# Reordering the start of a tuned graph-attention kernel: projections ahead of the mask rows, later weight loads, and a wider split of the last rows

## The chip, the cores and the metric

The kernel runs on one core of one Trainium2 chip. The metric is the device time of the whole kernel in microseconds (us); the profile's span is some 1.8 us shorter than the time of the same execution. Every timed run below is in the fast state, but for the single run of before_again, whose state is unknown. Single executions of one and the same kernel still scatter over some 3 to 16 us, so the first results are quoted as a median with its lowest and highest, and the later ones as a ratio with its interval. TensorE is also called PE, VectorE DVE, ScalarE ACT, GpSimd POOL and SyncE SP.

## The reference

Sixteen graphs of 1024 nodes share one adjacency matrix. Each goes through three transformer blocks with masked attention and then one graph-attention layer. Cut to what matters:

```python
def block(adj, h, Wq, Wk, Wv, Wo, bo, ...):          # three times; 8 heads of 16
    Q, K, V = (h @ W split into heads for W in (Wq, Wk, Wv))
    scores = einsum('bnhd,bmhd->bhnm', Q, K) / sqrt(16)
    scores = where(adj == 0, -inf, scores)
    x = layernorm(h + softmax(scores) @ V @ Wo + bo)
    return layernorm(x + relu(x @ W1 + b1) @ W2 + b2)

def last(x, adj, W, a_src, a_dst, ...):
    h = x @ W
    e = leaky_relu((h @ a_src)[:, :, None] + (h @ a_dst)[:, None, :], 0.2)
    return layernorm(softmax(where(adj == 0, -inf, e)) @ h + x)
```

x is 16 x 1024 x 128 in float32, adj 1024 x 1024 in int32.

## The kernel before

The 16 graphs times 3 layers are 48 blocks. A block has 32 score steps: head group (2) x query half (2) x key tile (8). One step makes two PSUM slots of scores; ACT takes one (exponential, then a product with the 0/1 mask on POOL), VectorE the other (it adds the mask, then ACT does the exponential); in three of eight key tiles VectorE takes both. The key and query projections are kept as a high and a low part, which DMA copies stack in four interleaved rows ("stack"). The parts that the change touches:

```python
def slot(dtype=F32):                     # three of these, for scores
    return psum.tile([P, N], dtype, tag="s", name="s", bufs=3)
def bank():                              # one of these, for projections and the rest
    return psum.tile([P, 512], F32, tag="t", name="t", bufs=1)
...
W = [load_layer(nc, nc.sync, const, a, 0, ("Wq", "Wk"))]          # in 64 B pieces
W[0].update(load_layer(nc, nc.scalar, const, a, 0, ("Wv", "bo")))
...
for t in range(NT):                      # the eight mask rows are fetched at once
    ...
    nc.sync.dma_start(ai, adj[t * P:(t + 1) * P, :])
def masks(t):                            # one mask row: DVE, 8 transposes, DVE, ACT
    ai, ab = rows_in[t]
    nc.vector.tensor_scalar(ab, ai, 0.0, None, op0=OP.not_equal)
    ps = slot(BF16)
    for k in range(NT):
        nc.tensor.transpose(ps[:, k * P:(k + 1) * P], ab[:, k * P:(k + 1) * P], identb)
    psv = ps.rearrange("p (k q) -> p k q", q=P)
    nc.vector.tensor_copy(mask01[:, :, t * P:(t + 1) * P], psv)
    nc.scalar.activation(mask_add[:, :, t * P:(t + 1) * P], psv, AF.Identity, scale=-BLOCKED, bias=blocked, ...)
def first_weights():                     # layer 0's other weights: ACT issues them
    W[0].update(load_layer(nc, nc.scalar, const, a, 0, ("Wo", "b2", "W1", "b1", "W2", "ln1_g", "ln2_g")))
    norm_weights(nc.scalar, 0)
    add_bias(nc.scalar, "ln1_b", 0, "b2", 0)
...
def rows_gh():                           # in the last layer of each batch
    ...
    for r in range(2):
        queue = nc.scalar if r and b == B - 1 else nc.sync
        for i in range(4):
            queue.dma_start(g_rows[...], parts[...])
            queue.dma_start(h_rows[...], parts[...])
...
put(proj_tasks(0), ("proj", 0))          # the start
need(("proj", 0))
for t in range(NT):
    masks(t)
stack(0, 0)
first_weights()
fetch(1)()
...
for m, (b, l) in enumerate(blocks):
    order = [(g, qh) for g in range(G) for qh in range(2)]
    if m == len(blocks) - 1:
        order.sort(key=lambda x: x[1])
    for at, (g, qh, kt) in ...:
        if at == 1:
            stack(m, 1)
        if n == 3:
            other_weights()
        ...
        if at == 19:
            need(("proj", m + 1)); stack(m + 1, 0)
        e = score_step(step)
```

Of the kernel before, what the change touches and what calls it, by code (L numbers as in the profile page):

```python
# [9 lines left out]
F32 = mybir.dt.float32  # L10
# [8 lines left out]
P = 128  # L19
H = 8  # L20
HD = 16
G = 2
# [6 lines left out]
SOON = 120  # L29
LANES = 4  # L30
AHEAD = 4
BOTH_ON_DVE = (2, 5, 7)
# [27 lines left out]

def load_layer(nc, queue, pool, a, l, names):
    w = {}
    for n in names:
        src = a[f"L{l}_gnn_{n}"]
        if n in ("Wq", "Wk"):

            t = pool.tile([P, src.shape[1]], F32, name=f"{n}{l}")
            for g in range(G):
                queue.dma_start(t.rearrange("p (g j d) -> p g j d", g=G, j=J)[:, g],
                                src.rearrange("i (j g d) -> i g j d", g=G, j=J)[:, g])  # L70
        elif n == "b1":
            t = pool.tile([P, src.shape[0] // P], F32, name=f"{n}{l}")
            queue.dma_start(t, src.rearrange("(f p) -> p f", p=P))
        elif n == "W2":
            t = pool.tile([P, src.shape[0] // P, src.shape[1]], F32, name=f"{n}{l}")
            queue.dma_start(t, src.rearrange("(f p) d -> p f d", p=P))
        elif len(src.shape) == 2:
            t = pool.tile([P, src.shape[1]], F32, name=f"{n}{l}")
            queue.dma_start(t, src)
        else:  # L80
            t = pool.tile([P, src.shape[0]], F32, name=f"{n}{l}")
            queue.dma_start(t, rows_of(src))
        w[n] = t
    return w
# [22 lines left out]
def fast_path(ctx: ExitStack, tc: tile.TileContext, a: dict, out: bass.AP, flag):  # L107
# [13 lines left out]
    def slot(dtype=F32):  # L121

        return psum.tile([P, N], dtype, tag="s", name="s", bufs=3)

    def bank():

        return psum.tile([P, 512], F32, tag="t", name="t", bufs=1)

    def half_tile(name):
# [13 lines left out]
    state = {("x", 0): load_x(0)}  # L143
    W = [load_layer(nc, nc.sync, const, a, 0, ("Wq", "Wk"))]
    W[0].update(load_layer(nc, nc.scalar, const, a, 0, ("Wv", "bo")))
# [22 lines left out]
    for t in range(NT):  # L168
        if t < 6:
            ai = work.tile([P, 2, N], I32, tag="e", name="ai", bufs=6)  # L170
            ai, ab = ai[:, 0], ai.bitcast(BF16)[:, 1, :N]
        else:
            ai = work.tile([P, N], I32, tag="Wk", name="ai", bufs=4)
            ab = work.tile([P, N], BF16, tag="Wq", name="ab", bufs=4)
        nc.sync.dma_start(ai, adj[t * P:(t + 1) * P, :])
        rows_in.append((ai, ab))

    def masks(t):
        ai, ab = rows_in[t]
        nc.vector.tensor_scalar(ab, ai, 0.0, None, op0=OP.not_equal)  # L180
        ps = slot(BF16)
        for k in range(NT):
            nc.tensor.transpose(ps[:, k * P:(k + 1) * P], ab[:, k * P:(k + 1) * P], identb)
        psv = ps.rearrange("p (k q) -> p k q", q=P)
        nc.vector.tensor_copy(mask01[:, :, t * P:(t + 1) * P], psv)
        nc.scalar.activation(mask_add[:, :, t * P:(t + 1) * P], psv, AF.Identity, scale=-BLOCKED, bias=blocked,
                             saturate=False)
# [14 lines left out]
    def first_weights():  # L202
        W[0].update(load_layer(nc, nc.scalar, const, a, 0, ("Wo", "b2", "W1", "b1", "W2", "ln1_g", "ln2_g")))
        norm_weights(nc.scalar, 0)
        add_bias(nc.scalar, "ln1_b", 0, "b2", 0)

# [4 lines left out]
    def other_weights():  # L211
        for l in range(1, L):
            W.append(load_layer(nc, nc.sync, const, a, l, [n for n in LAYER if n not in ("ln1_b", "ln2_b")]))
            norm_weights(nc.sync, l)
            add_bias(nc.sync, "ln2_b", l - 1, "bo", l)
            add_bias(nc.sync, "ln1_b", l, "b2", l)
        nc.sync.dma_start(ln2_b_last, rows_of(a[f"L{L - 1}_gnn_ln2_b"]))
        for n in LAST:
            src = a[f"L3_gnn_{n}"]
            if n == "W":  # L220
                t = w_nodes[:, :D]
                nc.sync.dma_start(t, src)
            elif n in ("a_src", "a_dst"):
                t = const.tile([P, 1], F32, name=n)
                nc.sync.dma_start(t, src.rearrange("(p o) -> p o", o=1))
            else:
                t = const.tile([P, D], F32, name=n)
                nc.sync.dma_start(t, rows_of(src))
            wl[n] = t

    def last_weights():
# [19 lines left out]
    def soon():  # L251

        return tc.high_priority(offset=SOON)

# [76 lines left out]
    def proj_tasks(m):  # L331
# [39 lines left out]
        return [(2 if n in (3, 4, 5, 6) else 1, f, {0: "+w", 1: "+w", 6: "-w", 7: "-w"}.get(n, "")) for n, f in enumerate(pieces)]  # L371

    def stack(m, g):

        for n, order in (("Wk", (0, 1, 0, 1)), ("Wq", (0, 0, 1, 1))):
            for pp in range(2):
                t = work.tile([P, N], F32R, tag=n, name=n, bufs=4)
                r0 = (g * J + 2 * pp) * HD
                for i, part in enumerate(order):
                    nc.sync.dma_start(t[i:P:4, :].bitcast(F32), state[n, m][part][r0:r0 + 2 * HD, :].bitcast(F32))  # L380
                state[n, g, pp] = t
# [5 lines left out]
    def score_step(step):  # L387
# [3 lines left out]
        for pp in range(2):  # L391
# [9 lines left out]
            if on_pool:  # L401
                nc.scalar.activation(ev, psv, AF.Exp, scale=HD ** -0.5)  # L402
                nc.gpsimd.tensor_mul(ev, ev, m)  # L403
            else:
                nc.vector.tensor_add(ev, psv, m)  # L405
                masked.append((2 * step_no[0] + pp + (kt not in BOTH_ON_DVE), ev))
# [106 lines left out]
    def last_tasks(b):  # L513
# [39 lines left out]
        def rows_gh():  # L553
# [6 lines left out]
            for r in range(2):  # L560

                queue = nc.scalar if r and b == B - 1 else nc.sync
                for i in range(4):
# [103 lines left out]

    put(proj_tasks(0), ("proj", 0))
    need(("proj", 0))
    for t in range(NT):  # L670
        masks(t)
    stack(0, 0)
    first_weights()
    fetch(1)()

# [44 lines left out]
    with tc.manual_schedule(engines={mybir.EngineType.PE, mybir.EngineType.Activation}):  # L720
        for m, (b, l) in enumerate(blocks):
            order = [(g, qh) for g in range(G) for qh in range(2)]
            if m == len(blocks) - 1:
                order.sort(key=lambda x: x[1])
            for at, (g, qh, kt) in enumerate((g, qh, kt) for g, qh in order for kt in range(NT)):
                now[0] = n
                if at == 1:
                    stack(m, 1)
                if n == 3:
                    other_weights()  # L730
                if n == 40:
                    last_weights()
                if at == 0 and m + 2 < len(blocks) and blocks[m + 2][1] == 0:
                    put([(0, fetch(blocks[m + 2][0]), "+x")], ("fetch", blocks[m + 2][0]))
                if m + 1 < len(blocks):
                    if at == 6:
                        need(("post",) + (blocks[m + 1][0], blocks[m + 1][1] - 1) if blocks[m + 1][1] else
                             ("fetch", blocks[m + 1][0]))
                        put(proj_tasks(m + 1), ("proj", m + 1), first=True)
                    if at == 19:  # L740
                        need(("proj", m + 1))
                        stack(m + 1, 0)
                step = m, g, qh, kt
                e = score_step(step)
                waiting.append((step, e, n + AHEAD))
# [249 lines left out]
```

## Time and profile before

| | before |
|---|---|
| time on record for the prediction, median of 3 | 4124.35 us (4121.5 to 4125.04) |
| profiled execution, span | 4126.3 us, granted clock 0.985 |
| first score on TensorE | 41.99 us |
| first masked sum on VectorE | 45.38 us |
| accumulator mark 1 (first transpose of the accumulator, 8 steps) | 68.98 us |
| accumulator mark 8 (end of the second block) | 196.79 us |
| "parts" of the last batch but one to the end of the span | 70.6 us |

The marks are the lines `tt<-acc` of the DVE timeline: VectorE turns over the accumulator once in eight steps, so equal marks of two kernels show how far one is ahead. The other names are of the last layer: "parts" is the small tile from which the rows of g and h are copied, the edges are TensorE's products of these rows, and an aggregate is 128 matmuls of edge weights with node values (`t<-hd,e`). The page's totals say how busy the engines are over all (busy us, share of the span, instructions):

```profile
PE 3819.7 (93%) x44501; PEld 1548.1 (38%) x44501; DVE 3405.9 (83%) x5324; ACT 3393.8 (82%) x3961; POOL 3445.7 (84%) x3010
```

With TensorE 93% busy and the middle nearly untouched (only the order of the copies in `stack` changes there, in every block), only the first and the last 70 us are in play. The prediction shows and reads the other lines.

### The profile page before, as it was taken

Reading aid. Unit: us, or ns where it says so; the run is one execution under the profiler, and the core shown is the slowest. Engines: PE = TensorE matmul, PEld = TensorE weight load, DVE = VectorE, ACT = ScalarE, POOL = GpSimd, SP = SyncE. Lnnn points to the kernel's source line nnn. Section 1 sums busy time; section 2 is a strip of 40 time slices with the busy share of each in tenths; the row PEclk is TensorE's granted clock in tenths of the full one; section 3 lists DMA queues with packets and bytes.
Section 4 is the critical chain, followed back from the end, with each engine's and each line's share of the span. In section 5 each row is a group of like instructions: output and inputs, shape, how many; then the busy total and the mean of one; then the engine's idle time right before and its main releaser. Section 6 shows DMA issues by size and latency. Waiting matters only on the chain.

```text
span 4126.3 us, 107667 instructions
## 1 busy us (share of the span) xinstructions
PE 3819.7 (93%) x44501; PEld 1548.1 (38%) x44501; DVE 3405.9 (83%) x5324; ACT 3393.8 (82%) x3961; POOL 3445.7 (84%) x3010
## 2 busy tenths in 40 slices
PE   7999999999999999999999999999999999999996
PEld 2333333344443333334444333333444433333445
DVE  6888888888887888888888888888888888888874
ACT  6899999977778999997777899998777789999760
POOL 4788888887788888897878888888888888888885
PEclk9999999999999999999999999999999999999998
DMA  5221221222221222221222212221222212212100
GB/s 152 68 57 47 63 62 43 62 53 53 54 66 50 62 52 53 62 54 47 68 53 53 63 47 58 62 56 50 53 60 63 52 42 63 62 48 57 45 25 19
DMA packets 126289, 233.11 MB, mean 56 GB/s; under 512 B 36704, under 2 KB 75616, under 8 KB 125792
## 3 DMA queue, kind: packets, MB, share of 16 engines
q1 hardware_dynamic: 122896, 225.14, 21.7%
q8 instruction: 352, 5.77, 0.6%
q10 hardware_dynamic: 2896, 1.01, 0.1%
q14 instruction: 145, 1.19, 0.1%
HBM read 15.54 MB, written 8.39 MB: 6 GB/s over the span
## 4 chain that ended last, share of the span: by engine, by line
PE 47%; DVE 19%; ACT 12%; POOL 12%; issue 9%; DMA 1%; SPq 0%; ACTq 0%; DVEq 0%; POOLq 0%
PE t L271 18%; PE acc L422 15%; PE s L395 11%; DVE e L405 11%; POOL e L403 6%; ACT e L402 5%; ACT e L417 5%; DVE st L296 2%; PE t L260 2%; POOL x L315 2%; DVE lo L360 2%; DVE x L303 1%; ACT xT L265 1%; DVE tt L433 1%; POOL x L319 1%
## 5 line engine op out<-in xcount | busy, mean ns | idle before, releaser
L405 DVE TENSOR_TENSOR e<-s,mask_add 128x1024 f32<-128x1024 f32 x2112 | 2500.1, 1212 | 413.3 <-PE s L395 328.0
L417 ACT ACTIVATE e<-e 128x1024 f32<-128x1024 f32 x2112 | 2196.4, 1062 | 364.1 <-DVE e L405 341.2
L403 POOL TENSOR_TENSOR e<-e,mask 128x1024 f32<-128x1024 f32 x960 | 2049.3, 2150 | 395.4 <-ACT e L402 392.7
L422 PE MATMUL acc<-e,v 128*17 128x512 f32 x12288 | 1630.9, 603 | 64.0 <-DVE tt L433 32.9
L395 PE MATMUL s<-Wq,Wk 64*128 64x512 f32 x6144 | 1209.0, 459 | 80.3 <-ACT e L402 34.9
L402 ACT ACTIVATE e<-s 128x1024 f32<-128x1024 f32 x960 | 982.3, 1023 | 188.3 <-PE s L395 172.2
L395 PEld LDWEIGHTS s<-Wq,Wk 64*128 64x128 f32 x6144 | 499.1, 186 | 1069.1 <-DVE e L405 437.2
L422 PEld LDWEIGHTS acc<-e,v 128*17 128x17 f32 x12288 | 208.0, 95 | 581.4 <-issue 463.8
L315 POOL TENSOR_SCALAR x<-x,mv 128x128 f32<-128x128 f32 x896 | 389.2, 448 | 24.0
L319 POOL TENSOR_TENSOR x<-x,ln_g 128x1024 f32<-128x1024 f32 x97 | 229.3, 2364 | 28.8 <-PE t L260 28.8
L271 PE MATMUL t<-hd,e 128*32 128x129 f32 x8192 | 245.6, 277 | 7.3 <-DVE x L597 3.2
L313 POOL TENSOR_TENSOR mv<-mv,half_neg 128x4 f32<-128x4 f32 x224 | 231.9, 1035 | 18.5
L271 PEld LDWEIGHTS t<-hd,e 128*32 128x32 f32 x8192 | 227.4, 111 | 27.0 <-issue 5.2
L271 PE MATMUL t<-x1T,W 128*32 128x512 f32 x1536 | 203.5, 602 | 3.1 <-ACT x1T L265 1.6
L303 DVE TENSOR_TENSOR x<-t,x 128x512 f32<-128x512 f32 x192 | 131.8, 686 | 89.8 <-PE t L271 84.5
L260 PE MATMUL t<-identf,x 128*128 128x128 f32 x896 | 150.9, 292 | 55.4 <-DVE lo L360 27.4
L296 DVE BATCH_NORM_STATS2 st<-x 128x6 f32<-128x128 f32 x896 | 196.8, 279 | 3.0
L271 PEld LDWEIGHTS t<-W,hT 128*32 128x32 f32 x6144 | 171.4, 110 | 62.5 <-issue 26.5
L311 POOL TENSOR_SCALAR mv<-mv 128x4 f32<-128x4 f32 x224 | 52.8, 236 | 167.5 <-DVE mv L298 137.4
L260 PEld LDWEIGHTS t<-identf,x 128*128 128x128 f32 x896 | 97.0, 144 | 251.9 <-issue 96.5
L271 PE MATMUL t<-W,hT 128*32 128x128 f32 x6144 | 185.4, 273 | 2.7 <-DVE x L303 1.9
L582 DVE SCALAR_TENSOR_TENSOR e<-s,mask 128x1024 f32<-128x1024 f32 x128 | 150.6, 1210 | 5.9 <-PE s L579 4.8
(83 smaller groups left out, 2490.1 us busy)
## 6 DMA issues: line engine op xcount, KB each, us to landing
Wk<-hi SPq DMA_DIRECT2D x384, 128.0 KB
Wk<-lo SPq DMA_DIRECT2D x384, 128.0 KB
Wq<-hi SPq DMA_DIRECT2D x384, 128.0 KB
Wq<-lo SPq DMA_DIRECT2D x384, 128.0 KB
x<-in_x_dram SPq DMA_DIRECT2D x16, 512.0 KB
out_dram<-x SPq DMA_DIRECT2D x31, 256.0 KB
ai<-in_adj_dram SPq DMA_DIRECT2D x8, 512.0 KB
g_rows<-parts SPq DMA_DIRECT2D x124, 4.0 KB
```

Of the source, the lines that this page charges most:

```text
L260: nc.tensor.transpose(ps[:, t * P:(t + 1) * P], src[:, 4 * h + t, :], identf)
L271: nc.tensor.matmul(dst[j:j + SLOT, :], lhsT[:, j:j + SLOT], rhs, start=start, stop=stop)
L296: nc.vector.bn_stats(st[:, t, :], z[:, t, :])
L313: nc.gpsimd.tensor_tensor(v, v, half_neg[:, ts], OP.pow)
L315: nc.gpsimd.tensor_scalar(z[:, t, :], z[:, t, :], mv[:, t, 0:1], mv[:, t, 1:2], op0=OP.add, op1=OP.mult)
L319: nc.gpsimd.tensor_mul(z, z, rows(gain, n))
L395: nc.tensor.matmul(ps[:, r * 512:(r + 1) * 512], k[64 * r:64 * r + 64, kt * P:(kt + 1) * P], q[64 * r:64 * r + 64, q0:q0 + 512], start=Tru ...
L402: nc.scalar.activation(ev, psv, AF.Exp, scale=HD ** -0.5)
L403: nc.gpsimd.tensor_mul(ev, ev, m)
L405: nc.vector.tensor_add(ev, psv, m)
L417: nc.scalar.activation(ev, ev, AF.Exp, scale=HD ** -0.5)
L422: nc.tensor.matmul(acc[j * SLOT:j * SLOT + HD + 1, :], v_bufs[m % 2][:, kt, 2 * j + g, :], e[:, j, :], start=first, stop=last)
```

## The change

Its intent: start the scores sooner. ACT loses the early weight loads; the first block's projections come first, in the three score slots; scores start with half of the queries and so half of the mask rows; the other four mask rows are made inside steps 1 to 4; all other weights load later from SP. A side change gives ACT half of the g and h rows of the last batch but one, as before only of the last. The core of the diff:

```diff
     def bank():
+        if head[0]:
+            return slot()[:, :512]
         return psum.tile([P, 512], F32, tag="t", name="t", bufs=1)
...
-    W = [load_layer(nc, nc.sync, const, a, 0, ("Wq", "Wk"))]
+    raw = {n: work.tile([P, D], F32, tag="row", name=n, bufs=2) for n in ("Wk", "Wq")}
+    W = [load_layer(nc, nc.sync, const, a, 0, ("Wk", "Wq"), raw)]     # whole rows, DVE reorders
...
-        W[0].update(load_layer(nc, nc.scalar, const, a, 0, ("Wo", "b2", "W1", "b1", "W2", "ln1_g", "ln2_g")))
-        norm_weights(nc.scalar, 0)
-        add_bias(nc.scalar, "ln1_b", 0, "b2", 0)
+        W[0].update(load_layer(nc, nc.sync, const, a, 0, ("Wo", "b2", "W1", "b1", "W2", "ln1_g", "ln2_g")))
+        norm_weights(nc.sync, 0)
...
     def stack(m, g):
-        for n, order in (("Wk", (0, 1, 0, 1)), ("Wq", (0, 0, 1, 1))):
-            for pp in range(2):
+        for pp in range(2):
+            for n, order in (("Wk", (0, 1, 0, 1)), ("Wq", (0, 0, 1, 1))):
...
-                queue = nc.scalar if r and b == B - 1 else nc.sync
+                queue = nc.scalar if r and b >= B - 2 else nc.sync
...
-    put(proj_tasks(0), ("proj", 0))
-    need(("proj", 0))
-    for t in range(NT):
-        masks(t)
-    stack(0, 0)
-    first_weights()
-    fetch(1)()
+        load_rows(range(4))
+        put(proj_tasks(0), ("proj", 0))
+        need(("proj", 0))
+        stack(0, 0)
+        load_rows(range(4, NT))
+        fetch(1)()
+        ...                                     # masks of rows 0 to 3
+    head[0] = False
...
-            if m == len(blocks) - 1:
+            if m in (0, len(blocks) - 1):
                 order.sort(key=lambda x: x[1])
-                if at == 1:
+                if at == (6 if m == 0 else 1):
                     stack(m, 1)
-                if n == 3:
-                    other_weights()
+                if n == 6:
+                    with tc.issue_after(behind["stack"]):
+                        first_weights()
+                        other_weights()
+                if n == 20:
+                    with tc.issue_after(behind["pool"]):
+                        biases()
-                    if at == 19:
+                    if at == (24 if m == 0 else 19):
                         need(("proj", m + 1))
                         stack(m + 1, 0)
-                e = score_step(step)
+                if FIRST <= n < FIRST + 4:
+                    with tc.manual_schedule(engines={mybir.EngineType.DVE}):
+                        e = score_step(step)
+                        neighbours(4 + n - FIRST)
+                        masks(4 + n - FIRST, mask_rows(4 + n - FIRST))
+                else:
+                    e = score_step(step)
```

## The prediction

> **What bounds the kernel now.** I read the 40 slices first (the page), then busy time by stretches, then the timeline at both ends. The slices say that TensorE is full almost everywhere:
>
> ```profile
> PE   7999999999999999999999999999999999999996
> ACT  6899999977778999997777899998777789999760
> ```
>
> Only the first slice (103 us) and the last have slack, and the change edits just these two. In between nothing moves: one block of 32 score steps lasts 217.18 to 293.31 us = 76.1 us between equal marks (the transposes of the accumulator), with TensorE busy 71.6 of them:
>
> ```profile
> 217.18 0.71 DVE L433 STREAM_TRANSPOSE tt<-acc 128x512 f32<-128x512 f32 x1
> ...
> 293.31 0.70 DVE L433 STREAM_TRANSPOSE tt<-acc 128x512 f32<-128x512 f32 x1
> ```
>
> So the time is start-up + a stream of fixed rate + drain, and the change can be worth no more than what it takes off the ends. The start, in stretches (columns: stretch, its length, busy us and count of PE, PEld, DVE, ACT, POOL, granted clock, DMA share, GB/s):
>
> ```profile
> 6.00:12.00 6.00, 0.48 (x3) 0.07 (x1) 0.00 (x0) 0.00 (x0) 0.00 (x0) 1.00 0.73 154
> 18.00:24.00 6.00, 3.21 (x22) 1.56 (x20) 3.75 (x4) 3.72 (x4) 2.75 (x2) 1.00 1.03 414
> 36.00:42.00 6.00, 3.82 (x68) 2.78 (x66) 0.69 (x1) 1.17 (x2) 0.00 (x0) 0.60 0.69 172
> 48.00:54.00 6.00, 5.25 (x18) 1.60 (x20) 4.36 (x4) 5.93 (x7) 4.10 (x3) 0.50 0.75 193
> 60.00:117.00 57.00, 54.80 (x438) 16.38 (x434) 49.74 (x52) 56.23 (x64) 42.06 (x25) 1.00 0.45 107
> ```
>
> Nothing computes until 12 us, though x lands at 5.4: the timeline shows ACT's first work, a table load, behind 14 weight loads that ACT issues.
>
> ```profile
> 13.39 1.28 ACT L263 ACT_TABLE_LOAD   x1 [13.39 <-DMA ln_gc<-in_L_gnn_ln_g_dram]
> 22.67 1.94 PE L271 MATMUL t<-xT,Wk 128*32 128x512 f32 x8
> 36.68 1.66 SPq L380 DMA_DIRECT2D Wq<-hi  x2
> 41.99 0.79 PE L395 MATMUL s<-Wq,Wk 64*128 64x512 f32 x2
> 45.38 5.75 DVE L405 TENSOR_TENSOR e<-s,mask_add 128x1024 f32<-128x1024 f32 x5 [8.01 <-PE s L395]
> 60.45 1.23 DVE L405 TENSOR_TENSOR e<-s,mask_add 128x1024 f32<-128x1024 f32 x1 [0.34 <-ACT e L417]
> ```
>
> Then eight mask rows sit between the projections, which have one PSUM bank (L271 waits for "lo" each time), 16 copies that stack hi and lo leave SP from 29.97 to 42.2 at some 0.64 us each, and the first masked sum on VectorE comes at 45.38. Eleven such sums are one run of eight steps, so 60.45 is step 8's. That is the mark I carry over.
>
> **What the Trainium skill says.** (1) "TensorE: Matmul & The Clock Gate", Part 1: the array starts at half rate, and an idle window of some 3.4 us sends it back. The trace agrees: eight projection matmuls took 1.94 us at 22.67 but 1.06 at 31.70, and the granted clock was 0.50 from 38 to 54 us. (2) Same page, "Architectural detail": ACT and DVE are strict FIFO. The table load at 13.39 agrees. (3) "DMA: Bandwidth & Descriptors", Specifications: under 512 B a transfer loses line rate. The trace agrees: 154 GB/s while Wq, Wk (64 B pieces) and the 4 B columns load, 414 GB/s when only mask rows are in flight. (4) Same page, "Issuing engines are not separate DMA queues": a second issuing engine saves only the time to issue. So the new split over ACT near the end can save issue time at most, and it spends ACT's.
>
> **The change, part by part.** I checked in the built order that the instructions stand as the diff suggests.
>
> *Weights later, Wq/Wk in whole rows.* ACT now issues 2 loads and can load its table at about 2 us. The transposes start at 5.4 as before; with 1.09 us each the xT copies are out by 8.2 (before: 19.6). Two DVE copies (about 0.25 us each, estimate from the 128x128 cast at 0.22) are added, before anything waits for DVE.
>
> *Projections first, in three slots.* TensorE cold: Wk 7.5 to 11.4 (2 x 1.94), Wq until about 14 (a slot returns 1.3 us after its matmuls: hi 0.58 + lo 0.68), V until about 17. Stacking starts at 12, the first eight copies (now those of one head pair, Wk and Wq) leave SP by 17.1 and land by 20 (the last one before took 2.83); the other eight leave by 22.2 and land by 25.
>
> *Four mask rows.* DVE is free at 15.3; neighbours 0.69, eight transposes 1.0, copy 0.69, ACT 1.11: rows 0 to 3 end on ACT at about 23.7. The first score is then at 22, and with the second head pair at 25 the first masked sum is at about 25.6. Against 45.38 that is **19.8 us gained**.
>
> *Four mask rows inside steps 1 to 4, DVE in fixed order.* Each adds to DVE 0.69 + 0.69, and DVE stands still between them while PE transposes (0.8 to 1.0). A step then costs sum 1.2 (2.4 when both go to DVE) + 0.69 + 0.1 + 0.9 + the larger of copy 0.69 and next scores 0.8 to 1.6: about 3.9, 4.9, 4.2, 4.2 us, against 1.84 before (14.7 us for eight). That is 17.2 against 7.4, **about 10 us given back**. Rows 4 to 7 leave SP at 22.3 and at 0.5 MB per 1.3 us (414 GB/s) land from about 26, just in time.
>
> *Stacking of the second head group at step 6 and halves by query.* The buffers of Wk and Wq are shared with mask rows 6 and 7, so these 16 copies start only when steps 3 and 4 have used them: about 38 and 43; the last lands at about 50.8. Step 8 needs them then. Step 8's sum comes at about 51, against 60.45: **net at the head -9.5 us**. The query halves are what allows a start with four rows (half 0 reads only mask rows 0 to 3; rows 4 to 7 are wanted at step 16), but they also bring the second head group forward from step 16 to 8. After it the stream runs as before; loads of later weights (50 issues at 0.47 = 24 us after 48) end before the next stacking at step 24, and that one (16 x 0.64 + 2.8 = 13 us) fits in eight steps of 1.88.
>
> *Rows of g and h for the last batch but one: half on ACT.* Before, these lines stood so:
>
> ```profile
> 4055.94 0.64 SPq L565 DMA_DIRECT2D g_rows<-parts  x1
> 4057.43 0.78 ACT L265 ACTIVATE xT<-t,ln_bc,ln_gc 128x512 f32<-128x512 f32 x1 [1.52 <-PE t L260]
> 4067.57 0.92 PEld L579 LDWEIGHTS s<-g_rows,h_rows 4*128 4x128 f32 x7 [0.83 <-DMA g_rows<-parts]
> 4069.42 1.47 ACTq L565 DMA_DIRECT2D g_rows<-parts  x1
> ```
>
> The edges wait for SP's 16 issues only from 66.46 to 67.6, some 1.1 us. In the new order eight issues stand on ACT right behind "parts" and ahead of the last batch's two xT copies. The last batch's eight took ACT from 4069.42 to 4076.3 = 6.9 us. So xT moves from 4057.4 to about 4062.5, and with it the node projections, which TensorE runs before those edges: the edges move from 67.6 to about 71.9. I take **+3.5 us at the tail**, a loss.
>
> Sum: 4124.35 - 9.5 + 3.5 = 4118.4. I put 4117, because the change was surely tuned with the fixed places in mind.
>
> **The rivals.** *(a) The whole 20 us stays.* If rows 4 to 7 hide in the slack of cold steps, the time is near 4105. For it: DVE had 2.62 of 6 us busy at 42 to 48. Against: the order is fixed and add, test, transpose, copy form one chain. *(b) The gain is eaten by a new wait*: the second group's copies land late (four loads of x, 2 MB, are queued ahead of them), or TensorE stays cold longer because the head is thinner; half rate for 8 us more costs about 3. Then the head gives 4 us and the sum is 4123. For it: the copies land within a microsecond of their use in my count. *(c) The tail is neutral or gains 1 us* if ACT issues faster than it did for the last batch, with 4113. *(d) ACT is the bound of the first block* (56.23 of 57 us at 60 to 117), so mask work moved into it must be paid in full: 4 x 1.11 = 4.4 us. That is inside the 10 I charge, not on top, as long as DVE's chain is longer.
>
> **Range and chances.** Head between -15 and -4, tail between -1 and +5, chip to chip about 2. That gives 4107 to 4125, with 4117 as the middle. Two per cent is 82 us; the whole start-up is 45 us, so faster by 2% is impossible short of a mistake of mine, and slower needs a new stall in every block, which the order does not show. Faster 0.01, within 0.98, slower 0.01.
>
> **What would show it.** Right: table load near 2 us, first Wk projection near 7.5, first masked sum near 25.6, the four steps with masks about 4.3 us each, step 8's sum near 51, equal block times of 76.1 after the first, and the last batch's xT some 5 us further from "parts" than 1.8. Wrong: step 8 before 46 (masks are hidden, rival a) or after 56 (rival b, with PE waiting for Wq copies); xT straight behind parts (rival c); or block times that differ from 76.1, which would mean that something I hold fixed has moved.

## The result, and the profile after

The changed kernel took 4121.23 us (median of 4 runs, 4115.92 to 4123.1); the kernel before, on the same chip, 4122.93 us (4 runs, 4120.17 to 4125.04). The ratio is 0.9994, with a 95% interval of 0.9977 to 1.0011: the same within 2%. (A ratio is the mean time of one kernel's fast runs over that of the other's of the same rounds, so it isn't quite the ratio of the medians quoted.) A second, longer measurement follows among the experiments: 0.9988.

The slices of the changed kernel are those of before but for ACT's first digit:

```profile
PE   7999999999999999999999999999999999999996
...
ACT  7999999977778999997777899998777789999760
```

Busy time of the changed kernel in the same stretches (stretch, length, busy us and count of PE, PEld, DVE, ACT, POOL, granted clock, DMA share, GB/s):

```profile
6.00:12.00 6.00, 6.00 (x34) 1.96 (x36) 1.85 (x5) 2.45 (x5) 2.36 (x1) 1.00 0.90 344
18.00:24.00 6.00, 1.04 (x10) 0.58 (x10) 1.15 (x2) 3.44 (x4) 2.12 (x1) 0.78 0.81 195
36.00:42.00 6.00, 3.81 (x21) 1.98 (x18) 3.42 (x5) 3.62 (x4) 2.15 (x1) 0.50 0.47 112
48.00:54.00 6.00, 6.00 (x44) 1.82 (x40) 5.44 (x6) 5.35 (x6) 2.15 (x1) 0.95 0.57 144
60.00:117.00 57.00, 54.36 (x458) 16.94 (x456) 51.66 (x55) 56.14 (x62) 43.15 (x28) 1.00 0.48 109
```

TensorE works from 6 us on (6.00 of 6 us, before 0.48), then does little from 18 to 24 us (1.04 of 6), and from 36 to 42 us it runs at half clock with neither DVE nor ACT full: that is where the mask rows stand inside the steps. (The clock column shows 1.00 until the first clock event in the trace, at 11.1 us here. The projections before it took 3.64 us for sixteen matmuls, the 1.82 for eight of a cold TensorE, so that 1.00 isn't to be believed.) The timeline of the changed kernel at the start (start, us, engine, line, what it writes and reads, in brackets the idle time before it and what ended it):

```profile
1.70 1.28 ACT L285 ACT_TABLE_LOAD   x1 [1.70 <-PEq L1029]
...
7.05 3.64 PE L293 MATMUL s<-xT,Wk 128*32 128x512 f32 x16
...
19.69 0.50 PE L419 MATMUL s<-Wq,Wk 64*128 64x512 f32 x2 [1.15 <-ACT mask_add L205]
25.53 1.65 PE L419 MATMUL s<-Wq,Wk 64*128 64x512 f32 x6 [5.34 <-DMA Wq<-lo]
```

and VectorE's through the steps with masks:

```profile
26.44 2.36 DVE L429 TENSOR_TENSOR e<-s,mask_add 128x1024 f32<-128x1024 f32 x2 [7.17 <-PE s L419]
28.71 1.85 DVE L193 TENSOR_SCALAR ai<-ai 128x1024 bf16<-128x1024 int32 x1
31.69 0.69 DVE L204 COPY mask<-s 128x1024 bf16<-128x1024 bf16 x1 [1.13 <-PE s L199]
32.42 2.36 DVE L429 TENSOR_TENSOR e<-s,mask_add 128x1024 f32<-128x1024 f32 x2
...
37.67 1.22 DVE L429 TENSOR_TENSOR e<-s,mask_add 128x1024 f32<-128x1024 f32 x1 [0.47 <-PE s L419]
...
41.78 1.23 DVE L429 TENSOR_TENSOR e<-s,mask_add 128x1024 f32<-128x1024 f32 x1 [0.47 <-PE s L419]
...
47.31 2.36 DVE L429 TENSOR_TENSOR e<-s,mask_add 128x1024 f32<-128x1024 f32 x2 [1.88 <-PE s L419]
49.95 1.22 DVE L429 TENSOR_TENSOR e<-s,mask_add 128x1024 f32<-128x1024 f32 x1 [0.28 <-PE s L419]
51.36 3.67 DVE L429 TENSOR_TENSOR e<-s,mask_add 128x1024 f32<-128x1024 f32 x3 [0.18 <-PE s L419]
```

The first sum comes at 26.44, where before had 45.38. Then each step with a mask row takes 4 to 5.5 us. Counting eleven sums, step 8's is the third of the last line, at about 53.8 (51.36 plus two of 1.22). At the first mark the lead of 18.9 has shrunk to 68.98 - 62.35 = 6.6 us. Later blocks last what they lasted:

```profile
209.10 0.70 DVE L457 STREAM_TRANSPOSE tt<-acc 128x512 f32<-128x512 f32 x1
...
285.22 0.70 DVE L457 STREAM_TRANSPOSE tt<-acc 128x512 f32<-128x512 f32 x1
```

285.22 - 209.10 = 76.1 us, as before. At the other end of the changed kernel:

```profile
4043.89 0.25 ACT L582 CAST parts<-t 16x128 fp32r<-16x128 f32 x1 [0.78 <-PE t L579]
...
4050.76 0.78 ACT L287 ACTIVATE xT<-t,ln_bc,ln_gc 128x512 f32<-128x512 f32 x1 [6.61 <-DMA g_rows<-parts]
...
4059.79 1.22 PE L603 MATMUL s<-g_rows,h_rows 4*128 4x256 f32 x8
```

The last batch's xT comes 6.9 us behind "parts" (before 1.8), and the edges 15.9 (before, one matmul at 10.8 and the other seven at 11.95). Yet "parts" to the end of the span is 4114.1 - 4043.9 = 70.2 us, no longer than the 70.6 of before: something behind the edges gave 4 us back.

The two profiled spans differ by 12.2 us and the medians by 1.7. So one pair of profiles can't be read as the effect of the change; this became the first thing to settle.

### The profile page after: what moved, and what is told of

Read it like the earlier page. It is cut to its first block, busy times and chain, and to the rows that moved or that the text cites. A ratio compares the mean times of both kernels' runs of the same rounds, so it can differ in the third digit from the quotient of the medians.

```text
span 4114.1 us, 107861 instructions
## 1 busy us (share of the span) xinstructions
PE 3809.8 (93%) x44501; PEld 1545.5 (38%) x44501; DVE 3405.7 (83%) x5326; ACT 3393.8 (82%) x3961; POOL 3445.6 (84%) x3010
## 4 chain that ended last, share of the span: by engine, by line
PE 49%; DVE 19%; ACT 12%; POOL 11%; issue 9%; ACTq 0%; DMA 0%; SPq 0%; DVEq 0%; POOLq 0%
PE t L293 19%; PE acc L446 15%; PE s L419 12%; DVE e L429 11%; POOL e L427 6%; ACT e L426 5%; ACT e L441 5%; DVE st L318 2%; PE t L282 2%; DVE lo L382 1%; POOL x L337 1%; DVE x L325 1%; ACT xT L287 1%; DVE tt L457 1%; POOL x L341 1%
```

## The experiments

My theory after the result: (1) the head gains what the first marks say, because the later weight loads free ACT and the projections go first, and loses most of it again to the masks inside the steps; (2) the wider split of the g and h rows costs 3 to 4 us; (3) the rest of the difference between spans is scatter. The rivals: the change gives nothing; the slots or the query halves, not the weight loads, make the gain; the split is neutral. Twelve runs were made, in three groups of four (two repeat the kernels before and after, one repeats a variant); those of one group ran on the same chip and share the runs of the kernel before (median 4124.72 us for the first group, 4123.17 for the second, 4122.16 for the third). All gave correct results.

| kernel | time, us (runs) | ratio to before, 95% interval | first sum | mark 1 | mark 8 | "parts" to end |
|---|---|---|---|---|---|---|
| before (first profile) | 4122.93 (4) | 1 | 45.38 | 68.98 | 196.79 | 70.6 |
| before_again | 4119.31 (1) | | 42.15 | 65.82 | 192.07 | 70.3 |
| after (first profile) | 4121.23 (4) | 0.9994 [0.9977, 1.0011] | 26.44 | 62.35 | 188.71 | 70.2 |
| after_again | 4118.07 (13) | 0.9988 [0.9980, 0.9997] | 25.08 | 60.75 | 188.64 | 70.1 |
| tail_undo | 4116.29 (21) | 0.9980 [0.9973, 0.9987] | 25.41 | 60.95 | 188.82 | 66.9 |
| split_only | 4127.01 (12) | 1.0007 [0.9999, 1.0016] | 41.38 | 64.88 | 192.63 | 73.2 |
| weights_only | 4116.65 (20) | 0.9979 [0.9972, 0.9986] | 35.93 | 59.63 | 185.87 | 70.1 |
| weights_early | 4121.41 (12) | 0.9993 [0.9985, 1.0002] | 30.64 | 66.70 | 194.64 | 70.2 |
| one_bank | 4125.97 (12) | 1.0005 [0.9997, 1.0014] | 33.27 | 68.26 | 198.01 | 70.1 |
| pieces | 4123.76 (12) | 1.0005 [0.9996, 1.0013] | 25.28 | 61.11 | 188.60 | 70.0 |
| rows_ahead | 4108.48 (7) | 0.9967 [0.9956, 0.9978] | 28.66 | 52.04 | 182.03 | 70.6 |
| rows_ahead_tail | 4104.96 (5) | 0.9959 [0.9946, 0.9973] | 29.04 | 52.46 | 180.97 | 67.4 |
| rows_ahead_tail2 (the same again) | 4107.97 (6) | 0.9968 [0.9956, 0.9980] | 28.74 | 52.33 | 181.43 | 67.0 |
| rows_ahead_gmajor_tail | 4112.65 (21) | 0.9977 [0.9971, 0.9984] | 28.62 | 52.19 | 185.97 | 67.1 |

### The two kernels once more: before_again, after_again

No edit.

> The kernel before, nothing edited, for a second profile of its start. The kernel of the tail split alone has the very same start, yet its first masked sum came at 41.38 us and its eighth accumulator mark at 192.63, where the profiled run of the kernel before had 45.38 and 196.79: there VectorE waited for a late mask row. If the start of the kernel before scatters like this with the landing of the mask rows, this profile lies between 41 and 46 us with its first sum, and the head's gain of the change is some 4 to 8 us, not 8. If 45.38 is the rule and 41.38 was chance, it lies at 45 again.

> The changed kernel, nothing edited, timed in five rounds to tighten its ratio, and profiled once more. My reading of the first pair is that head -8.1 us and tail +3.9 us are what the change itself does, and that some 3.4 us came back behind the edges because even gaps of the instruction stream vanished in the last aggregates. Theory: the same first mark of the accumulator transposes (62.35 +- 0.5) and eighth mark (188.71 +- 1), parts to next xT 6.9 us, parts to end 70.2 to 70.8; time 4 to 9 us under the kernel before of the same rounds (ratio 0.9979 to 0.9990). Rival 'the change gives nothing': ratio 1.000 +- 0.0004 over five rounds.

The kernel before starts its masked sums at 42.15 in this profile, and mark 1 is at 65.82:

```profile
42.15 5.75 DVE L405 TENSOR_TENSOR e<-s,mask_add 128x1024 f32<-128x1024 f32 x5 [8.42 <-PE s L395]
```

The kernel split_only has the same start, and had 41.38. So 45.38 was a late one. In that profile the fourth mask row landed late, VectorE's test of it then fell on a product of POOL's and took 2.06 us instead of 0.69, and TensorE stood idle for it (first fence, kernel before), where split_only, with the same instructions, already had Wk's projection running (second fence):

```profile
19.92 2.06 DVE L180 TENSOR_SCALAR ai<-ai 128x1024 bf16<-128x1024 int32 x1 [1.42 <-DMA ai<-in_adj_dram]
22.03 0.71 PE L183 MATMUL s<-identb,ai 128*128 128x128 bf16 x5 [2.79 <-DVE ai L180]
```

```profile
20.38 1.94 PE L271 MATMUL t<-xT,Wk 128*32 128x512 f32 x8
```

The start of the changed kernel varies less: 26.44, 25.08 and 25.41 (tail_undo) at the first sum, and 188.71, 188.64 and 188.82 at mark 8. Against the two starts of before that weren't late (192.07 and 192.63, mean 192.35) the head of the change gains 3.6 us, not the 8.1 of the first pair. How often a start of before is late isn't known from three profiles; with all three (mean 193.8) the gain would be 5.1. I had expected mark 1 within 0.5 us of 62.35, and it came at 60.75. That mark 8 agrees so well is partly luck: between marks 4 and 5 the clock was halved for 3.4 us in after_again (24.45 us from mark to mark) and not in the first profile (22.91), which made up the difference. So a mark of one profile is good to some 1.5 us. The ratio of after_again, 0.9988 with an interval up to 0.9997, narrowly rules out that the change gives nothing.

The stretch from mark 8 to "parts" carries the same 46 blocks in every kernel. It took 3855.18 us in the first profile of the changed kernel and 3862.68 in the second (4043.89 - 188.71 and 4051.32 - 188.64), at granted clocks of 0.984 and 0.982 over the whole run; in all fourteen profiles it lies between 3855 and 3863. That is the scatter, and it is twice the effect of the change. The busy times of the stretch (first line after, second after_again) show where it sits:

```profile
188.71:4043.89 3855.18, 3608.12 (x41941) 1449.90 (x41941) 3230.14 (x5055) 3236.01 (x3775) 3294.07 (x2873) 0.99 0.22 54
188.64:4051.32 3862.68, 3615.91 (x41941) 1454.43 (x41941) 3230.78 (x5055) 3236.55 (x3775) 3294.34 (x2873) 0.99 0.22 54
```

The same 41941 matmuls took TensorE 7.8 us longer, and DVE, ACT and POOL were busy for what they were before. Counted from the clock events in the kept traces, the clock was halved for 69.9 us of the first stretch and 87.0 of the second, mostly for 3.4 us at a time; over the fourteen profiles the length of the stretch follows that time (correlation 0.94). Why the clock drops more often in one execution isn't shown. Ratios over many runs average the scatter as far as it is chance; a pair of spans does not.

### The tail: tail_undo, split_only

```diff
-                queue = nc.scalar if r and b >= B - 2 else nc.sync     # tail_undo: in the changed kernel
+                queue = nc.scalar if r and b == B - 1 else nc.sync
```

> The changed kernel with the rows of g and h of the last batch but one issued by SP alone, as before. Marks: distance from that batch's 'parts' cast to the next xT copy on ACT, and from 'parts' to the end of the span (before 1.8 and 70.6 us, changed kernel 6.9 and 70.2 us). My theory (eight issues on ACT hold the last batch's xT): 1.8 us again, edges of that batch some 4 us earlier after 'parts', and parts-to-end 66 to 67 us, so the whole about 3.5 us faster than the changed kernel. Rival (the tail is paced by the 128-matmul aggregates and their fetches, and xT is not what ends it): 1.8 us again but parts-to-end stays at 70 to 71, time equal to the changed kernel. The head marks (first masked sum 26.4, first accumulator transpose 62.4) stay in both.

split_only is the reverse edit in the kernel before.

> The kernel before with only the split of the g and h rows over SP and ACT for the last batch but one as well. Theory of the tail: head as before (first mark 68.98, eighth 196.8, within 1 us), parts to next xT 6.9 us instead of 1.8, parts to first edges 15.9 instead of 11.9, parts to end 74 (70.6 + 3.5), time +3.5 us, ratio 1.0008. If the gaps of the instruction stream behind the edges (3.4 us in the kernel before) are tied to where the edges fall and not to the head's code, they vanish here as they did in the changed kernel and parts to end stays near 70.5. Rival c of the prediction (tail neutral, or a gain of 1 us): xT at 1.8, end at 69.5 to 70.6.

With the split undone in the changed kernel, xT follows "parts" by 1.8 us again:

```profile
4045.45 0.26 ACT L582 CAST parts<-t 16x128 fp32r<-16x128 f32 x1 [0.78 <-PE t L579]
...
4047.23 0.78 ACT L287 ACTIVATE xT<-t,ln_bc,ln_gc 128x512 f32<-128x512 f32 x1 [1.52 <-PE t L282]
```

and the way to the end is 66.9 us instead of 70.2. With the split alone added to the kernel before, xT comes 6.9 us behind "parts" and the way to the end is 73.2 instead of 70.6 and 70.3. The four combinations:

| "parts" to end, us | SP alone | half on ACT |
|---|---|---|
| start of the kernel before | 70.6, 70.3 | 73.2 |
| start of the changed kernel | 66.9 | 70.2, 70.1 |

The split costs 3.3 us in the changed kernel and 2.8 in the kernel before (along the rows), whatever the start; rows_ahead and its two versions with the old split, below, give 3.2 and 3.6. The start changes the tail by 3.0 to 3.6 us (along the columns), whatever the split. "Start" stands here for everything in the change but the split, the order of the copies in `stack` included. The times agree, though their intervals would allow no effect too: tail_undo lies 3.3 us below the changed kernel by their differences to before (0.0020 and 0.0012 of 4123), split_only 2.9 us above before.

How can the start change the tail? The last aggregates of the kernel before have holes for which the profile shows no wait, marked "issue", in runs of 95 and 33 matmuls:

```profile
4103.07 2.86 PE L271 MATMUL t<-hd,e 128*32 128x129 f32 x95 [0.36 <-DVE x L597]
4106.67 1.16 PE L271 MATMUL t<-hd,e 128*32 128x129 f32 x33 [0.74 <-issue]
4108.82 2.86 PE L271 MATMUL t<-hd,e 128*32 128x129 f32 x95 [1.00 <-DVE x L597]
4112.43 1.19 PE L271 MATMUL t<-hd,e 128*32 128x129 f32 x33 [0.74 <-issue]
```

In the changed kernel the same 128 matmuls go through in one piece:

```profile
4093.11 3.75 PE L293 MATMUL t<-hd,e 128*32 128x129 f32 x128 [0.36 <-DVE x L621]
4097.89 3.75 PE L293 MATMUL t<-hd,e 128*32 128x129 f32 x128 [1.02 <-DVE x L621]
```

The last six aggregates take 3.87 to 4.79 us in the kernel before and 3.75 or 3.76 in the changed one. That makes 3.4 us, of which the marked holes are 2.1 (0.36, 0.27 and twice 0.74); the rest lies between matmuls that the view merges. The holes stand at the same matmul (95 and 33) in before_again and in weights_only, and two matmuls later (97 and 31) in split_only; no profile with the changed kernel's start shows them there. So they are not chance: they go with the instructions of the kernel, and the new start moved or removed them. What makes them I couldn't test. A guess is that the instructions themselves arrive late, and the traces speak for it: the last two holes stand 33 + 95 = 128 matmuls apart, with a weight load each 256 instructions; counted through the trace, they stand at the same two TensorE instructions in before, before_again, weights_only and split_only; and the queue that the page calls "instruction" brings pieces of 16 KiB (352 of them, 5.77 MB), here one in about 5 us. But the changed kernel has such transfers too, and no holes, so the cause stays open.

### The weights alone, and everything but the weights: weights_only, weights_early

weights_only is the kernel before with a single step of the change (at step 3 instead of 6, with the bias of layer 0 among them):

```diff
     def first_weights():
-        W[0].update(load_layer(nc, nc.scalar, ...)); norm_weights(nc.scalar, 0); add_bias(nc.scalar, ...)
+        W[0].update(load_layer(nc, nc.sync, ...)); norm_weights(nc.sync, 0); add_bias(nc.sync, ...)
...
-    first_weights()                      # at the start
...
                 if n == 3:
+                    first_weights()
                     other_weights()
```

> The kernel before with one part of the change alone: the weights of layer 0 that are not needed at once are issued by SP at step 3 instead of by ACT at the start. If the ACT queue's weight loads are what delays the head: table load at 1.7 us instead of 13.4, first xT copy near 6.5 instead of 14.7, first masked sum at 35 to 38 instead of 45.4, first accumulator transpose 59 to 62 instead of 69.0, time about 8 us less than before. Rival (mask rows arriving late, the single PSUM bank and the interleaved masks set the pace): table load at 1.7 but first masked sum only 2 to 4 us earlier, at 41 to 43.

weights_early is the changed kernel with that step taken back: seven of these loads issued by ACT at the start again, and the four loads of columns with them (the expectation says that these stay late, but in the trace ACT issues them from 6.98 to 9.5 us).

> The changed kernel with the loads of layer 0's other weights back on ACT's queue at the start (only the four loads of columns stay late). Theory: ACT issues seven more loads ahead of its table load, at about 0.7 us each in the kernel before, so table load at 6 to 9 us rather than 1.7, and with it the first xT copy, the first projection (7.05 becomes 9 to 12), the first masked sum (26.44 becomes 29 to 32) and the first accumulator mark (62.35 becomes 65 to 68). If instead the table load does not matter because x, Wk and the transfers set the first projection, the first masked sum stays within 1 us of 26.44.

weights_only starts its sums 6.2 us before before_again and keeps all of it to mark 8 (192.07 - 185.87 = 6.2):

```profile
35.93 5.75 DVE L405 TENSOR_TENSOR e<-s,mask_add 128x1024 f32<-128x1024 f32 x5 [7.26 <-PE s L395]
...
59.63 0.70 DVE L433 STREAM_TRANSPOSE tt<-acc 128x512 f32<-128x512 f32 x1
```

This one edit gives 0.9979, where the whole change gives 0.9988; their intervals overlap. In weights_early the table load waits behind the loads again, and with it the first projection (11.51 against 7.05 us):

```profile
9.58 1.28 ACT L285 ACT_TABLE_LOAD   x1 [9.58 <-DMA W<-in_L_gnn_W_dram]
```

Its first sum is 4.2 to 5.6 us later than the changed kernel's, its mark 8 is 5.9 later. So by the marks the weights that ACT need not issue are worth about 6 us with either start, and the other parts of the change together cost 188.7 - 185.9 = 2.8 us at mark 8 (1.2 in after_again at mark 4, before the halved clock). The times show this less well: weights_only is 8.7 us below before, but weights_early only 2 us above after_again (0.9993 and 0.9988), with an interval that holds both 0 and 6.

### The slots and the whole rows: one_bank, pieces

```diff
     def bank():                                                        # one_bank
-        if head[0]:
-            return slot()[:, :512]
```

> The changed kernel with the first block's projections in the one PSUM bank instead of the three slots of the scores; all else as changed. Theory: each of the eight fills then waits for hi and lo of the one before it (1.3 us), so V ends 4 to 7 us later and TensorE's 5 us of idle before the second head pair of scores is partly used up by that; but the copies that stack hi and lo (SP, 16 at about 0.64 us) are what the scores wait for, and they follow Wq: first masked sum 29 to 32 instead of 26.44, first accumulator mark 64 to 67. Rival: the slots do nothing because SP's copies set the first scores; first masked sum then within 1 us of 26.44.

```diff
-    W = [load_layer(nc, nc.sync, const, a, 0, ("Wk", "Wq"), raw)]      # pieces
+    W = [load_layer(nc, nc.sync, const, a, 0, ("Wk", "Wq"))]
```

> The changed kernel with layer 0's Wk and Wq fetched in 64 B pieces, as before, instead of whole rows that VectorE reorders; all else as changed. Theory: 4096 pieces are slow (154 GB/s over all while they load, in the kernel before) and delay the mask rows and x behind them; Wk lands at about 8 to 9 us instead of before 7, so the first projection, the first masked sum (25.1 to 26.4) and the first mark (60.75 to 62.35) move 1 to 3 us later. Rival: x, which lands at 5.4, and the cold projections set the start, and the pieces cost under 0.5 us.

In one_bank every projection waits for the low part of the one before it:

```profile
12.26 1.93 PE L291 MATMUL t<-xT,Wk 128*32 128x512 f32 x8 [1.43 <-DVE lo L380]
```

It costs more than I wrote: the first sum is at 33.27 (expected 29 to 32), mark 1 at 68.26 (expected 64 to 67), and mark 8 is 9.3 us later than in the changed kernel. With projections ahead of the masks nothing fills these waits of 1.43 us, and TensorE is cold (1.93 us for eight matmuls); the kernel before had its mask transposes in them. The new order needs the slots.

The 64 B pieces cost nothing at the start: first sum 25.28, mark 1 at 61.11, mark 8 at 188.60, all within 0.4 us of after_again. My theory of 1 to 3 us fell, and the rival holds: x and TensorE's cold projections set the start. (The two weights come in 2048 pieces, not the 4096 of my expectation.) The time of pieces, 4123.76 us, is nevertheless not below that of before, though its profiled span (4121.5) equals after_again's (4121.4) and its tail too. The difference lies in the middle stretch, where the profiles show 3862.93 and 3862.68, and there it goes with the clock: the twelve executions of pieces had a granted clock of 0.982 on average, before had 0.985 in the same rounds, and within pieces the time runs from 4115.01 us at 0.985 to 4127.52 at 0.981. On this chip, then, the lower clock goes with the kernel; whether the 64 B pieces make it or the changed kernel would have had it here too isn't shown. Differences of a few us between the times of two kernels can therefore be the clock's; the marks at both ends are the better evidence.

### The masks ahead of the scores: rows_ahead, rows_ahead_tail, rows_ahead_tail2

The changed kernel, but all eight rows loaded and masked before the first score, and the second group stacked at step 1:

```diff
-        load_rows(range(4))
+        load_rows(range(NT))
         ...
-        load_rows(range(4, NT))
-        for t in range(5): ...           # masks of four rows
+        for t in range(NT + 1): ...      # masks of all eight
...
-                if at == (6 if m == 0 else 1):
+                if at == 1:
                     stack(m, 1)
...
-                if FIRST <= n < FIRST + 4:
+                if False:
```

> The changed kernel, but all eight mask rows are loaded ahead of the stacking copies and masked before the first score; steps 1 to 4 carry no mask work, and the second head group is stacked at step 1. The changed kernel leaves DVE, PE and ACT idle from about 20.6 to 25.5 us while the stacking copies land. My theory (the chain test-transpose-copy inside steps 1 to 4 costs about 10 us and the idle stretch can hold it): first masked sum still at 26 to 27 us, first accumulator transpose at 52 to 54 instead of 62.4, end of the second block 8 to 10 us earlier than 188.7; time 4110 to 4114. Rival 1 (2 MB more of rows ahead of the copies in the same rings): first masked sum at 30 to 32, first transpose at 57 to 59, gain 4 us. Rival 2 (the steps are slow because of the cold clock, not because of masks): first transpose at 60 or later.

rows_ahead_tail has the tail's edit of tail_undo as well, and rows_ahead_tail2 is the same kernel again.

> Both edits above in one kernel. My theory: gains add, head as in rows_ahead and tail as in tail_undo; 4106 to 4111 us, 12 to 17 us under the kernel before. If either theory falls, the sum lacks that part: 4110 to 4117.

> The best version so far once more, over five rounds, beside the one without query halves: all eight mask rows ahead of the scores, and SP alone for the last batch but one's rows of g and h. Expected as in its first run: first mark 52.4, eighth 181, parts to next xT 1.8, parts to end 67 us, time 4103 to 4108, 15 to 19 us under the kernel before (ratio 0.9955 to 0.9965).

The sums start 2 to 4 us later than in the changed kernel (I had expected 26 to 27), but then eight steps run as fast as anywhere, five sums in one go:

```profile
28.66 5.82 DVE L429 TENSOR_TENSOR e<-s,mask_add 128x1024 f32<-128x1024 f32 x5 [1.75 <-PE s L419]
...
52.04 0.70 DVE L457 STREAM_TRANSPOSE tt<-acc 128x512 f32<-128x512 f32 x1
```

From first sum to mark 1 it is 52.04 - 28.66 = 23.4 us here, 23.6 and 23.7 in the two profiles of before, 23.7 in weights_only, but 62.35 - 26.44 = 35.9 and 35.7 in the two of the changed kernel. So four mask rows inside the steps cost 12.2 us there, and the same four rows ahead of the scores only the 2 to 4. The edit moves the stacking too, but in the changed kernel TensorE was busy for all of 48 to 54 us, so it did not wait for those copies at step 8. A cold TensorE (rival 2) isn't the cause by itself: here too the clock is halved from 23.2 to 36.9 us, across the five sums. But in the changed kernel it is halved from 21.3 to 48.6, so part of the 12.2 us is that longer cold time. At mark 8 rows_ahead is 6.6 us ahead of the changed kernel, less than the 8 to 10 expected. Together with the old tail it beats both kernels: 4104.96 and 4107.97 us, ratios 0.9959 and 0.9968, some 13 to 17 us under the kernel before. Even this is under 0.5%.

### The query halves: rows_ahead_gmajor_tail

rows_ahead_tail with the old order of the first block, so one head group for all queries and then the other:

```diff
-            if m in (0, len(blocks) - 1):
+            if m == len(blocks) - 1:
                 order.sort(key=lambda x: x[1])
...
-                    if at == (24 if m == 0 else 19):
+                    if at == 19:
```

> All eight mask rows ahead of the scores, with the kernel before's order of head groups and its split of the g and h rows: so no query halves in the first block. With the masks out of the steps the halves only decide whether the second head group's copies (16 on SP) are wanted at step 8 (halves) or at step 16. Theory: the copies are issued at step 1 in either order and land before step 8, so the halves are worth nothing here: first masked sum 28.5 to 29.5, first accumulator mark 52 to 53.5, time within 2 us of its twin with halves (some 4105). Rival: the copies of the second group are late for step 8, then this order is 2 to 4 us faster; or the projections of the second block, needed at a fixed step, interfere, then it is slower.

A miss. Mark 1 is as expected (52.19), but mark 8 is 4.5 us later than with the halves, and the time 4.7 us longer. The loss falls between marks 4 and 5. There POOL waits for rows of biases, whose loads stand on SP behind the stacking now issued at step 19, and VectorE then waits for POOL's product:

```profile
100.53 0.46 POOL L219 TENSOR_TENSOR b<-b,row 128x128 f32<-128x128 f32 x1 [3.18 <-DMA row<-in_L_gnn_ln_b_dram]
102.02 0.46 POOL L219 TENSOR_TENSOR bo<-bo,row 128x128 f32<-128x128 f32 x1 [1.03 <-DMA row<-in_L_gnn_ln_b_dram]
```

```profile
109.79 0.71 DVE L473 STREAM_TRANSPOSE aT<-A 128x512 f32<-128x512 f32 x1 [5.20 <-POOL A L460]
```

With the halves these rows arrive by 81 us, while POOL is less pressed. So the run says nothing for or against the halves as such; it suggests that the step at which the biases load was tuned to them, which a run with the biases moved would have to show.

## Why the prediction was right, and where its terms were off

The verdict, the range and most mechanisms held, though the total owes something to luck. 4117 us was predicted, in a range of 4107 to 4125; 4121.23 and 4118.07 were measured. Term by term:

- **Table load near 2 us, Wk at 7.5, first sum at 25.6.** Measured 1.70, 7.05, and 26.44 and 25.08. Right, and weights_early shows that the table load is what moves them. The gain was 18.9 us in the pair predicted from; against the usual 41.4 to 42.2 it is some 16.
- **Mask rows in the steps give back about 10 us.** Right in kind, too small: 12.3 us at step 8 in the first pair (53.8 - 26.44 = 27.4 against 60.45 - 45.38 = 15.1; the prediction writes 14.7 for the latter), and rows_ahead shows it by taking them out. The four steps were put at 3.9, 4.9, 4.2, 4.2 = 17.2 us. By the starts of the sums they took 4.8 (the second sum of the first line starts 1.14 after 26.44), 5.25, 4.1, 5.5 = 19.7. Two terms are missing. In the first step VectorE's test of neighbours took 1.85 us, not 0.68, with POOL's product in the way:

```profile
27.89 2.12 POOL L427 TENSOR_TENSOR e<-e,mask 128x1024 f32<-128x1024 f32 x1 [4.17 <-ACT e L426]
```

  It ends at 30.01, and the test, begun at 28.71, at 30.56. The late start of before has the same: a test of 2.06 us, ended 0.56 after POOL's product. The Trainium skill has this in "SBUF — State Buffer", Who interferes with whom: VectorE's `tensor_scalar` can take the port pair it shares with GpSimd, and whoever comes second is blocked for the other's whole instruction. The trace agrees. In the last step TensorE, still cold, first does an older step's product with V (profile of after_again):

```profile
43.27 1.91 PE L446 MATMUL acc<-e,v 128*17 128x512 f32 x8
45.11 1.06 PE L419 MATMUL s<-Wq,Wk 64*128 64x512 f32 x4
```

  and VectorE waits 1.88 us for the scores behind it. I had counted only copy or scores there.
- **Step 8 at 51.** Measured 53.8 and 52.2: the term above. Rivals (a) and (b) had set 46 and 56 as their marks; neither came. ACT as the bound, rival (d), did not come either: at 36 to 42 us it was busy 3.62 of 6.
- **Net head -9.5 us.** The step that was mis-sized most. The pair's own marks say -6.6 (mark 1) and -8.1 (mark 8); against the two starts of before that weren't late it is -3.6 at mark 8. I had taken 60.45 of one profile as the kernel's start, and it was some 3 us late by chance (57.3 in before_again, counting its sums in the same way).
- **Blocks of 76.1 us after the first, and a stream of fixed rate.** The block shown is right: 76.1. But the stream isn't fixed: its 46 blocks vary by 7.8 us with the time at half clock, which the prediction left out. Nor does the change touch the ends only, as I wrote: the order of the copies in `stack` is new in every block.
- **Tail +3.5 us, through ACT's issues ahead of xT.** Mechanism and size right: xT at +6.9 as written, 3.3 us by tail_undo and 2.8 by split_only. Rival (c) is out. What I did not foresee is that the new start takes 3.0 to 3.6 us, holes above all, out of the tail, which hides the loss in the total.
- **The sum.** Predicted -9.5 + 3.5 = -6. Measured -3.6 (head) + 3.1 (split, mean of its two measurements) - 3.3 (holes, mean of the columns) = -3.8; the medians say -1.7 and -5.1. The head was 5.9 us too good and the holes gave 3.3 back, so the errors partly cancel: the total came out better than its terms deserved, and that is luck.

And where the expected gain went: of the 16 us by which the sums start earlier than usual, 12 go to mask rows in the steps. One part of the change, the weights, gave about 6 us by itself.

## What to carry to other kernels

Work taken out of the start and put into the first steps isn't gone: inside a step with a fixed order every link of its chain (test, transpose, copy) is paid in full and with TensorE cold, so compare the time to a mark some steps later, not to the first step. Moving transfers off an engine's queue is the cheapest thing to try alone, and here it gave at least as much as the package that contained it. Before reading a few us out of two profiles, profile the same kernel twice, learn which stretches repeat, and compare the granted clocks.

## What the Trainium skill lacked or had wrong

- "DMA: Bandwidth & Descriptors", Issuing engines are not separate DMA queues: it calls the time to issue "usually small relative to the DMA itself" and gives no figure for the engine that takes the issues. Here eight small ones held ACT from 4044.18 to 4050.7 us (1.48 for the first, 0.61 to 0.70 for the others) and cost the kernel 2.8 to 3.3 us.
- Same page, Specifications: in 64 B pieces, under the 512 B that it asks for, Wk and Wq do lower the rate (250 GB/s from 6 to 8 us in pieces, 346 in after_again), but they cost the start under 0.4 us (mark 1 at 61.11 against 60.75), because x and the cold projections set it. Size alone doesn't say whether a transfer matters.
- "TensorE: Matmul & The Clock Gate": I found no figure for how much the gate makes a kernel scatter that is nearly always busy. The same 46 blocks took 3855.18 and 3862.68 us in two executions of one program, with 69.9 and 87.0 us at half clock.
- "Runtime: NRT & Kernel Launch", Instruction fetch mechanics: it has instructions come in blocks of 256 and calls the cost of crossing a block "mostly hidden". If the holes in TensorE's stream are that cost (they fit a distance of 256 instructions, but this wasn't tested), it isn't hidden here: 0.19 to 0.74 us each at the end of four profiles.
